# Two sets and two rounds in one tick of a fused convolution kernel

## The chip, the cores and the metric

The kernel runs on one core of a Trainium2 chip. The metric is the device time of one execution in microseconds (us), the median of several runs. The engines of a core are named as in the profile: PE (TensorE, matrix products), PEld (its weight loads), DVE (VectorE), ACT (ScalarE), POOL (GpSimd) and SP (SyncE, which here only starts transfers). All data are float32.

## The reference

The input `x` has 8 elements of 8 channels of 512x512. Two layers are computed, each added to its input. `_gn` is a normalisation over groups of two channels.

```python
x = x + _L0_conv_ref(_gn(x), T, X, weights1_ri, weights2_ri)   # spectral
x = x + _L1_conv_ref(_gn(x), K_local, Wp, bp, Wu, bu, Wg1, bg1, Wg2, bg2)

# layer 1, cut
grid = drive = x
for _ in range(15):                                  # STEPS
    mapped = 3.9 * grid * (1.0 - grid)
    local = conv3x3_depthwise(mapped, K_local)
    grid = 0.85 * (0.7 * mapped + 0.3 * local) + 0.15 * drive
cml_out = clip(grid, 0.0001, 0.9999)
h = relu(conv3x3(x, Wp, bp))                         # 8 -> 128 channels
nca_out = sigmoid(conv1x1(h, Wu, bu))                # 128 -> 8
gin = concatenate([x, cml_out, nca_out])
g = sigmoid(conv1x1(relu(conv3x3(gin, Wg1, bg1)), Wg2, bg2))
return g * cml_out + (1.0 - g) * nca_out
```

Layer 0 takes a few low frequencies of every second point of `x`, mixes the channels by weights and sums the waves back at all 512x512 points.

## The kernel before

The work of an element is cut into four kinds, which are interleaved in **ticks**. The order of the instructions on each engine is the order of the source (a helper, `keep_order`, fixes it).

- A **set** is one of the 15 steps for a fifth of the rows of half the channels. An element has 150 sets: 75 of its first half, 75 of its second. `convolve` does its products on PE, `settle` empties the two pairs of PSUM banks on DVE and squares the result on ACT. Every third step `renew` copies the rows that neighbouring slabs share. A set comes again five sets later.
- A **round** is 4 rows of the hidden layer: products from `cols`, relu to `h` (half on ACT, half on DVE), then the pointwise product, whose result is added up in `y` over four rounds. An element has 128 rounds.
- A **gate** is 12 rows of the last part, `conv` and `point`, for the element before the current one. There are 43 for an element.
- The **spectral pieces** compute layer 0 and the normalisation of the element after the current one. `layer0` is a generator and each `yield` ends a piece.

PSUM is four `pairs` of banks. A tick of before is one set (two pairs), one round (the other two), then a gate's conv, or its point, or up to two spectral pieces, and the round's pointwise product:

```python
pairs = [pp.tile([P, 2, N], F32, name=f"pair{i}") for i in range(4)]

def convolve(m, c0, step, ps):                       # L497
    for n, dx in enumerate((1, 0, 2)):
        for t in range(4):
            for h in range(4):
                at = slice(32 * h, 32 * h + 32)
                nc.tensor.matmul(
                    ps[h // 2][32 * t : 32 * t + 32, h % 2],
                    band[at, c0 + (t if step % 2 else h), dx],
                    m[at, t, dx : dx + N],
                    start=(n == 0), stop=(n == 2), tile_position=(32 * h, 32 * t),
                )

def settle(half, step, k, ps):                       # L552, L556
    m, d = half.m[k], half.d[k, step % 2]
    u = m[:, :, 1 : N + 1]
    for q in range(2):
        at = slice(2 * q, 2 * q + 2)
        nc.vector.scalar_tensor_tensor(
            u[:, at], ps[q], FLOOR, d[:, at], ALU.max, ALU.add
        )
        if step < STEPS:
            nc.scalar.square(u[:, at], u[:, at])
    # ... cut: a set's first and last steps, later(1, renew)

class Hidden:
    def round(self, ps, after):                      # L599, L605, L606
        # ... cut: which cols, the next load
        for n, (dx, lo, hi, at) in enumerate(SHIFTS):
            for g in range(4):
                p = slice(32 * g, 32 * g + 32)
                nc.tensor.matmul(
                    ps[g // 2][:, g % 2, lo:hi], w_p[p, dx, i % 2],
                    self.cols[p, i // 2, at : at + hi - lo],
                    start=(n == 0), stop=(n == 2), tile_position=(32 * g, 0),
                )
        self.h = wk.tile([P, 4, N], F32, tag="h", name="h", bufs=1)
        nc.scalar.activation(self.h[:, :2], ps[0], AF.Relu, bias=b_p)
        nc.vector.tensor_scalar(self.h[:, 2:], ps[1], b_p, 0.0, ALU.add, ALU.max)

    def point(self, ps):                             # L612, L618, L620
        i = self.n % 4
        for g in range(4):
            nc.tensor.matmul(
                ps[32 * g : 32 * g + 32], w_u[:, i], self.h[:, g],
                start=True, stop=True, tile_position=(0, 32 * g),
            )
        if i == 0:
            self.y = wk.tile([P, N], F32, tag="y", name="y", bufs=2)
            nc.scalar.copy(self.y, ps)
        else:
            nc.vector.tensor_tensor(self.y, self.y, ps, ALU.add)
        # ... cut: after four rounds sigmoid and store of y

class Gate:
    def conv(self, ps):                              # L662 on PE
        # ... 12 products of gin, tile_position=(0, 32 * j)
        # POOL: d - ng (L667); DVE: x1 (L668), relu of ps into mix (L672)
    def point(self, ps):                             # L677
        # one product; ACT: sigmoid (L678); POOL: d * g (L680); later(1, self.finish)
    def finish(self):                                # L686
        # DVE: one sum of three terms into mix; later(1, self.store)

def work(step, more, e, after, ps):
    if step:
        half, n, k = step
        convolve(half.m[k], half.c0, n - 1, ps[0])
        settle(half, n, k, ps[0])
    if more:
        e.hidden.round(ps[1], after)
    others.pieces([pair[:, 0] for pair in ps[0 if more else 1]])
    if more:
        e.hidden.point(ps[1][0][:, 0])
    tick()
```

`later(n, f)` runs `f` at the end of the n-th tick. Within an element all gates come first, the spectral pieces after them. The last element has only 48 rounds in its ticks with sets, and the rest of its rounds and its own gates follow in a tail without sets. Tiles of `sets` (15 slots) and `shared` (5 slots: `gin` and `mix` of gates, `x` of spectral pieces) are handed out by name.

Of the kernel before, what the change touches and what calls it, by code (L numbers as in the profile page):

```python
# [41 lines left out]
P = 128  # L42
# [12 lines left out]
ROUNDS, ROUNDS_LAST = 128, 48  # L55
SLAB, HALO, SETS = 32, 3, 5
SHARED = 5

# [66 lines left out]
def conv_layers(ctx: ExitStack, tc: tile.TileContext, a, out):  # L125
# [29 lines left out]
    def row(shape, name):  # L155
        return wk.tile(shape, F32, tag="row", name=name, bufs=3)
# [58 lines left out]
    def wave_table(name, pos, col, shift):  # L215
# [6 lines left out]
        u = row([8, N], "u")  # L222
# [8 lines left out]
        t = cp.tile([8, N], F32, name=name)  # L231
        nc.scalar.activation(t, u, AF.Sin, scale=6.283185)
        return t

    e1c = wave_table("e1c", "X", 0, 0.25)
    e1s = wave_table("e1s", "X", 0, None)
    e2 = wave_table("e2", "T", 1, waves[:, 2:3])


# [41 lines left out]
    def group_stats(st, n, bank):  # L281
# [5 lines left out]
        yield  # L287
# [8 lines left out]
        yield  # L296
# [6 lines left out]
        yield  # L303
        return mean, rstd, std

    def layer0(e, bank):

# [18 lines left out]
        yield  # L326
        mean, rstd, _ = yield from group_stats(st, G, bank)
# [9 lines left out]
        wmix = row([8, 2, C, C, 4], "wmix")  # L337
        nc.sync.dma_start(out=wmix, in_=a["wmix"])
        yield
# [10 lines left out]
        yield  # L350


        def total(q0, v0, q1, v1, op, name):
            ts = row([8, 2, C, C, 4], "ts")
            for i, (q, v) in enumerate(((q0, v0), (q1, v1))):
                nc.vector.tensor_tensor(
                    ts[:, i], f[:, :, q].unsqueeze(2).to_broadcast([8, C, C, 4]), wmix[:, v],
                    ALU.mult,
                )
            nc.vector.tensor_tensor(ts[:, 0], ts[:, 0], ts[:, 1], op)  # L360
            t = sm.tile([8, C, 4], F32, name=name)
            nc.vector.tensor_reduce(t, ts[:, 0].rearrange("k i o m -> k o m i"), AX.X, ALU.add)
            return t

        re = total(0, 0, 1, 1, ALU.subtract, "re")
        yield
        im = total(0, 1, 1, 0, ALU.add, "im")
        om = sm.tile([8, C, 2, 8], F32, name="om")
        s = 1.0 / (NS * NS)
        nc.vector.tensor_scalar(om[:, :, 0, 0:4], re, s, None, ALU.mult)  # L370
        nc.vector.tensor_scalar(om[:, :, 0, 4:8], im, s, None, ALU.mult)
        nc.vector.tensor_scalar(om[:, :, 1, 0:4], im, -s, None, ALU.mult)
        nc.vector.tensor_scalar(om[:, :, 1, 4:8], re, s, None, ALU.mult)
        yield


        def over_rows(c):
            ps = bank[-1]
            nc.tensor.matmul(ps[:8], om[:, c, 0], e1c, start=True, stop=False)
            nc.tensor.matmul(ps[:8], om[:, c, 1], e1s, start=False, stop=True)  # L380
# [6 lines left out]
        def close(g, st):  # L387

            mean, rstd, std = yield from group_stats(st, 1, bank)
            nc.vector.tensor_copy(means[:, 0, g : g + 1], mean)  # L390
            nc.vector.tensor_copy(means[:, 1, g : g + 1], std)
            for c in (2 * g, 2 * g + 1):
# [10 lines left out]
                yield  # L403
# [3 lines left out]
        closing = iter(())  # L407
        for c in range(C):
# [3 lines left out]
            for j in range(4):  # L412
# [3 lines left out]
                nc.vector.bn_stats(st[:, c % 2, j], xt[:, j])  # L416
                yield
                if j == 2 and c + 1 < C:
                    ty_next = over_rows(c + 1)
                    yield  # L420
                if next(closing, closing) is not closing:
                    yield
            if c % 2:
                closing = close(c // 2, st)
            if c + 1 < C:
                yield C + c + 1
        for _ in closing:
            yield
        back = e.back
# [3 lines left out]
        nc.vector.tensor_reduce(back, pick, AX.X, ALU.add)  # L433
# [7 lines left out]
    class Half:  # L441
# [22 lines left out]
        def prepare(self, n):  # L464

            for k in range(SETS):
                if n == k - 2:
                    self.square(k)
                if n == 2 * k - 5:
                    self.drive(k, 1)  # L470
            while n >= -10 and self.loads and (self.loads[0][2] or sets.free):
# [57 lines left out]
    def leave(m, k, half):  # L529
# [14 lines left out]
        later(2, store)  # L544

    def settle(half, step, k, ps):
# [3 lines left out]
        for q in range(2):  # L550
# [3 lines left out]
            )  # L554
            if step < STEPS:
# [12 lines left out]
    class Hidden:  # L568
# [4 lines left out]
        def __init__(self, e):  # L573
            self.e, self.tiles, self.loaded, self.n = e, deque(), 0, 0
# [12 lines left out]
        def round(self, ps, after):  # L587

            i = self.n % 4
# [14 lines left out]
            self.h = wk.tile([P, 4, N], F32, tag="h", name="h", bufs=1)  # L604
            nc.scalar.activation(self.h[:, :2], ps[0], AF.Relu, bias=b_p)  # L605
            nc.vector.tensor_scalar(self.h[:, 2:], ps[1], b_p, 0.0, ALU.add, ALU.max)  # L606

        def point(self, ps):

            i = self.n % 4  # L610
            for g in range(4):
                nc.tensor.matmul(  # L612
                    ps[32 * g : 32 * g + 32], w_u[:, i], self.h[:, g],
                    start=True, stop=True, tile_position=(0, 32 * g),
                )
            if i == 0:
                self.y = wk.tile([P, N], F32, tag="y", name="y", bufs=2)
# [3 lines left out]
            self.n += 1  # L621
            if i == 3:
                y, r0 = self.y, 4 * self.n - 16
# [10 lines left out]
    class Gate:  # L634
# [39 lines left out]
        def point(self, ps):  # L674
# [6 lines left out]
            later(1, self.finish)  # L681

        def finish(self):
# [5 lines left out]
            later(1, self.store)  # L689
# [12 lines left out]
    class Element:  # L702


        def __init__(self, b):
            self.b, self.rows = b, 0
            self.xn, self.cml, self.nca = planes[b % 2]
# [23 lines left out]
        def spectral(self, ps):  # L731

            if not self.pieces:
                return
            if self.need is not None and now[0] < self.at.get(self.need, now[0]) + 3:
                return
            self.bank.append(ps)
            self.need = next(self.pieces, self)
            if self.need is self:
                self.pieces = None  # L740
            self.bank.clear()

    class Others:


        def __init__(self):
            self.before, self.after, self.limit = None, None, 2
            self.loaded, self.convolved = deque(), deque()

        def feed(self):  # L750
            e = self.before
            while e and e.gates and len(self.loaded) < self.limit and len(shared.free) > 1:
# [5 lines left out]
            if self.after and not (e and e.gates):  # L758
                self.after.fetch()

        def busy(self):
            return self.before.gates or self.loaded or self.convolved

        def pieces(self, banks):

            if self.convolved:
                self.convolved.popleft().point(banks[0])
            elif self.loaded and self.loaded[0].at + 2 <= now[0]:
                self.convolved.append(self.loaded.popleft())
                self.convolved[0].conv(banks[0])  # L770
            elif self.after:
                for ps in banks:
                    self.after.spectral(ps)
# [5 lines left out]
    for i in range(2):  # L779
# [11 lines left out]
    for c, t in enumerate(xs_first):  # L791
        e.x[c], e.at[c], e.at[C + c] = t, -3, -3
    turns = cycle(pair[:, 0] for pair in pairs)
    while e.pieces:
        e.spectral(next(turns))
# [3 lines left out]
    for n in range(-10, 0):  # L799
# [5 lines left out]
    def work(step, more, e, after, ps):  # L805

        if step:
            half, n, k = step
            convolve(half.m[k], half.c0, n - 1, ps[0])
            settle(half, n, k, ps[0])  # L810
        if more:
            e.hidden.round(ps[1], after)
        others.pieces([pair[:, 0] for pair in ps[0 if more else 1]])
        if more:
            e.hidden.point(ps[1][0][:, 0])
        tick()

    halves = pairs[:2], pairs[2:]
    for b in range(B):
        after = Element(b + 1) if b + 1 < B else None  # L820
        others.after = after
        rounds = ROUNDS if after else ROUNDS_LAST
        for t in range(2 * TICKS):
            half, behind = (e.first, e.second) if t < TICKS else (e.second, after and after.first)
            n = t % TICKS
            assert not after or t != 2 * TICKS - 10 or not after.pieces
            half.prepare(n)
            if behind:
# [72 lines left out]
```

## Time and profile before

| | before |
|---|---|
| time, median of 3 runs | 11553.06 us (11540.5 to 11559.4) |
| span of the profiled run | 11555.9 us |
| first product of a set | 238.7 us after the start |
| end of the last set | 11037.5 us |
| mean granted PE clock | 0.974 |
| transferred | 1353.10 MB, mean 117 GB/s |

A group line of the profile names the line of the source, the engine, the operation, the output and inputs, and the count. Then come the busy time and the mean length of one in ns, and then the engine's idle time just before these instructions with what ended most of it. A timeline line has the start in us, the length, the engine and the instruction. Products overlap in PE, so the time that a block of them takes is read from its start to the start of the next block. 1200 sets and 1024 rounds are spread over the 11.5 ms.

### The profile page before, as it was taken

What the parts mean: (1) busy time and instruction counts of PE and PEld (TensorE: products, weight loads), DVE (VectorE), ACT (ScalarE), POOL (GpSimd) and SP (SyncE); (2) the same over time, 40 slices, a digit from 0 to 9 for tenths busy, and PEclk for the clock granted to TensorE, in tenths of its full rate; (3) what the DMA queues carried; (4) which work ended last, traced back from release to release, by engine and by line L of the source; (5) the groups of instructions that cost most, each with busy time, mean ns of one, the idle gap of its engine ahead of it and who ended that gap; (6) DMA issues with size and microseconds to landing.
All of it is one profiled execution on the core that took longest, in us unless ns stands there. A gap on an engine that the chain in (4) does not pass through costs nothing. (4 is left out here: it accounts for less than half of the span.)

```text
span 11555.9 us, 349769 instructions
## 1 busy us (share of the span) xinstructions
PE 10228.8 (89%) x158864; PEld 3755.7 (33%) x158864; DVE 6597.8 (57%) x6779; ACT 4243.8 (37%) x4444; POOL 1733.2 (15%) x1285
## 2 busy tenths in 40 slices
PE   5988889899898989989899898988989899897789
PEld 2332233233333333333333333333333233332222
DVE  4654456566565655656565655656656566555455
ACT  1333333334333334334333333433433334333322
POOL 0010021300113011120112102121021200122012
PEclk9999999999999999999999999999999999999999
DMA  3222045632556335562355514564145632555067
GB/s 107 85 72 60 29 126 135 158 108 75 139 130 161 102 99 126 130 163 82 112 126 138 161 64 121 130 152 137 60 130 134 162 109 72 148 140 135 20 167 179
DMA packets 624855, 1353.10 MB, mean 117 GB/s; under 512 B 72452, under 2 KB 72580, under 8 KB 593356
## 3 DMA queue, kind: packets, MB, share of 16 engines
q1 hardware_dynamic: 559712, 1161.94, 38.3%
q10 hardware_dynamic: 63660, 168.77, 5.9%
q8 instruction: 1249, 20.46, 0.8%
q14 instruction: 234, 1.92, 0.1%
HBM read 992.29 MB, written 268.66 MB: 109 GB/s over the span
## 5 line engine op out<-in xcount | busy, mean ns | idle before, releaser
L497 PE MATMUL pair<-m,band 32*32 32x512 f32 x115200 | 4462.1, 617 | 249.3 <-DVE m L552 140.3
L556 ACT ACTIVATE m<-m 128x1024 f32<-128x1024 f32 x2240 | 2365.9, 1057 | 5188.4 <-DVE m L552 4866.4
L599 PE MATMUL pair<-cols,w_p 32*128 32x511 f32 (+1 forms) x24576 | 2933.7, 606 | 32.8 <-ACT mix L678 18.2
L497 PEld LDWEIGHTS pair<-m,band 32*32 32x32 f32 x115200 | 1797.5, 104 | 2877.1 <-issue 1454.9
L552 DVE SCALAR_TENSOR_TENSOR m<-pair,dO 128x1024 f32<-128x1024 f32 x1280 | 1507.1, 1219 | 1517.1 <-PE pair L497 1361.2
L552 DVE SCALAR_TENSOR_TENSOR m<-pair,dE 128x1024 f32<-128x1024 f32 x1120 | 1318.8, 1219 | 1267.4 <-PE pair L497 1177.1
L612 PE MATMUL pair<-h,w_u 128*32 128x512 f32 x8192 | 1177.3, 625 | 856.5 <-ACT h L605 855.4
L599 PEld LDWEIGHTS pair<-cols,w_p 32*128 32x128 f32 x24576 | 1163.1, 185 | 1819.2 <-issue 1606.8
L606 DVE TENSOR_SCALAR h<-pair,b_p 128x1024 f32<-128x1024 f32 x1024 | 1313.1, 1282 | 551.8 <-PE pair L599 496.0
L605 ACT ACTIVATE h<-pair,b_p 128x1024 f32<-128x1024 f32 x1024 | 1126.0, 1100 | 911.4 <-PE pair L599 509.3
L680 POOL TENSOR_TENSOR mix<-mix 96x512 f32<-96x512 f32 x344 | 437.8, 1273 | 4765.0 <-ACT mix L678 3929.8
L662 PE MATMUL pair<-gin,w_g 128*32 128x511 f32 (+1 forms) x8256 | 982.9, 609 | 54.5 <-DVE m L552 52.7
L560 POOL TENSOR_SCALAR dO<-dO 128x2048 f32<-128x2048 f32 x80 | 436.2, 5452 | 3945.5 <-DVE m L552 3945.5
L620 DVE TENSOR_TENSOR y<-y,pair 128x512 f32<-128x512 f32 x768 | 526.3, 685 | 833.7 <-PE pair L612 826.5
L686 DVE SCALAR_TENSOR_TENSOR mix<-mix,back 96x512 f32<-96x512 f32 x344 | 619.6, 1801 | 395.5 <-POOL mix L680 350.5
L612 PEld LDWEIGHTS pair<-h,w_u 128*32 128x32 f32 x8192 | 197.5, 110 | 1618.9 <-ACT h L605 1453.2
L662 PEld LDWEIGHTS pair<-gin,w_g 128*32 128x32 f32 x8256 | 238.3, 111 | 751.0 <-issue 467.1
L667 POOL TENSOR_TENSOR mix<-mix 96x512 f32<-96x512 f32 x344 | 441.8, 1284 | 162.2 <-DMA mix<-nca 80.9
L677 PE MATMUL pair<-mix,w_g 128*96 128x512 f32 x688 | 379.1, 633 | 7.0 <-DVE mix L672 7.0
L624 ACT ACTIVATE y<-y,b_u 128x512 f32<-128x512 f32 x256 | 184.8, 722 | 524.2 <-DVE y L620 524.1
L672 DVE TENSOR_SCALAR mix<-pair,b_g 128x512 f32<-128x512 f32 x344 | 257.1, 747 | 159.4 <-PE pair L662 156.4
L668 DVE SCALAR_TENSOR_TENSOR mix<-mix,back 96x512 f32<-96x512 f32 x344 | 308.3, 896 | 0.0
(85 smaller groups left out, 2943.1 us busy)
## 6 DMA issues: line engine op xcount, KB each, us to landing
gin<-xn SPq DMA_DIRECT2D x344, 384.0 KB
cols<-xn SPq DMA_DIRECT2D x256, 512.0 KB
x<-in_x SPq DMA_DIRECT2D x120, 1024.0 KB
gin<-cml SPq DMA_DIRECT2D x344, 320.0 KB
gin<-nca SPq DMA_DIRECT2D x344, 320.0 KB
dE<-xn ACTq DMA_DIRECT2D x320, 256.0 KB
dO<-xn ACTq DMA_DIRECT2D x320, 256.0 KB
mix<-xn SPq DMA_DIRECT2D x344, 192.0 KB
```

What stands on the lines that cost most here:

```text
L497: nc.tensor.matmul(ps[h // 2][32 * t : 32 * t + 32, h % 2], band[at, c0 + (t if step % 2 else h), dx], m[at, t, dx : dx + N], start=(n == ...
L552: nc.vector.scalar_tensor_tensor(u[:, at], ps[q], FLOOR, d[:, at], ALU.max, ALU.add)
L556: nc.scalar.square(u[:, at], u[:, at])
L599: nc.tensor.matmul(ps[g // 2][:, g % 2, lo:hi], w_p[p, dx, i % 2], self.cols[p, i // 2, at : at + hi - lo], start=(n == 0), stop=(n == 2), ...
L605: nc.scalar.activation(self.h[:, :2], ps[0], AF.Relu, bias=b_p)
L606: nc.vector.tensor_scalar(self.h[:, 2:], ps[1], b_p, 0.0, ALU.add, ALU.max)
L612: nc.tensor.matmul(ps[32 * g : 32 * g + 32], w_u[:, i], self.h[:, g], start=True, stop=True, tile_position=(0, 32 * g),)
L620: nc.vector.tensor_tensor(self.y, self.y, ps, ALU.add)
L662: nc.tensor.matmul(ps[32 * j : 32 * j + 32, lo:hi], gband[:, dx], gin[:, j, at : at + hi - lo], start=(n == 0), stop=(n == 2), tile_positi ...
L667: nc.gpsimd.tensor_tensor(d, d, ng, ALU.subtract)
L680: nc.gpsimd.tensor_tensor(d, d, mix[: GR * C, 2], ALU.mult)
L686: nc.vector.scalar_tensor_tensor(o, o, self.e.back[: GR * C, 0:1], x1, ALU.add, ALU.add)
```

## The change

A tick becomes two sets, each with its own two pairs of banks, then two rounds, then the gate or the spectral pieces, then the two pointwise products, and at the end the gate's point or more spectral pieces. An element has 75 ticks, 64 of them with rounds. It is meant to let the work that empties one block's banks lie beside the next block's products.

`settle` is now a generator, so that the relu of the first round is placed before the second square of the second set on ACT. The gate's last sum (`finish`) comes in the following tick after the eviction of a set, and its store at once. Gates are loaded until tick 27 of an element, then the spectral pieces run from tick 26 on, and the remaining gates follow, so that no gates stand in the middle of an element; for that there are three sets of planes in DRAM instead of two. `h` has two buffers, `y` one and `row` two instead of three. The two products of `over_rows` are merged into one. Pieces are marked `LATER` (the first in its group only) or `LONG` (two large ones per tick at most).

```diff
+GATES_TO, SPECTRAL_FROM = 27, 26
+LONG, LATER = -1, -2
...
-        return wk.tile(shape, F32, tag="row", name=name, bufs=3)
+        return wk.tile(shape, F32, tag="row", name=name, bufs=2)
...
         def over_rows(c):
             ps = bank[-1]
-            nc.tensor.matmul(ps[:8], om[:, c, 0], e1c, start=True, stop=False)
-            nc.tensor.matmul(ps[:8], om[:, c, 1], e1s, start=False, stop=True)
+            nc.tensor.matmul(ps[:8], om[:, c], e1, start=True, stop=True)
...
-        later(2, store)
+        later(1, store)
     def settle(half, step, k, ps):
...
             )
+            if q:
+                yield
             if step < STEPS:
                 nc.scalar.square(u[:, at], u[:, at])
...
-            self.h = wk.tile([P, 4, N], F32, tag="h", name="h", bufs=1)
-            nc.scalar.activation(self.h[:, :2], ps[0], AF.Relu, bias=b_p)
-            nc.vector.tensor_scalar(self.h[:, 2:], ps[1], b_p, 0.0, ALU.add, ALU.max)
+            h = wk.tile([P, 4, N], F32, tag="h", name="h", bufs=2)
+            nc.scalar.activation(h[:, :2], ps[0], AF.Relu, bias=b_p)
+            next(settled, None)
+            nc.vector.tensor_scalar(h[:, 2:], ps[1], b_p, 0.0, ALU.add, ALU.max)
+            self.hs.append((self.n - 1, h))
...
-                self.y = wk.tile([P, N], F32, tag="y", name="y", bufs=2)
+                self.y = wk.tile([P, N], F32, tag="y", name="y", bufs=1)
...
-            later(1, self.finish)
...
-            later(1, self.store)
+            self.store()
...
-            self.xn, self.cml, self.nca = planes[b % 2]
+            self.xn, self.cml, self.nca = planes[b % 3]
...
+        def feed(self, t):
+            e, after = self.before, self.after
+            spectral = after and after.pieces
+            while e and e.gates and (t < GATES_TO or not spectral):
...
+        def first(self, banks):
+            self.longs = 0
+            n = 0
             if self.convolved:
-                self.convolved.popleft().point(banks[0])
-            elif self.loaded and self.loaded[0].at + 2 <= now[0]:
-                self.convolved.append(self.loaded.popleft())
-                self.convolved[0].conv(banks[0])
+                self.point(banks[1])
+                n = 2
+            if self.loaded and self.loaded[0].at < now[0]:
+                g = self.loaded.popleft()
+                g.conv(banks[0])
+                self.convolved.append(g)
+                n = n or 1
+            elif n == 0 and self.after:
+                n = self.spectral(banks)
+            return n
+
+        def second(self, banks, wait):
+            if self.convolved:
+                if not wait:
+                    self.point(banks[0])
             elif self.after:
-                for ps in banks:
-                    self.after.spectral(ps)
+                self.spectral(banks)
...
+    def work(sets, rounds, e, after):
+        settled = iter(())
+        for (half, step, k), ps in zip(sets, (pairs[:2], pairs[2:])):
+            convolve(half.m[k], half.c0, step - 1, ps)
+            next(settled, None)
+            settled = settle(half, step, k, ps)
+            next(settled)
+            others.finish()
+        others.finish()
+        for ps in (pairs[:2], pairs[2:])[:rounds]:
+            e.hidden.round(ps, after, settled)
+        next(settled, None)
+        a, b, c, d = (pair[:, 0] for pair in pairs)
+        n = others.first([a, b])
+        if rounds:
+            e.hidden.point(c if n else a)
+        if rounds > 1:
+            e.hidden.point(d if n else c)
+        others.second([pair[:, 1] for pair in pairs[2:]], rounds == 0)
         tick()
```

## The prediction

> **What bounds the kernel now.** I read the busy shares first, then the costliest groups, then who waits for whom, and last single ticks in the timeline.
>
> ```profile
> PE 10228.8 (89%) x158864; PEld 3755.7 (33%) x158864; DVE 6597.8 (57%) x6779; ACT 4243.8 (37%) x4444; POOL 1733.2 (15%) x1285
> ```
>
> TensorE (PE) is busy 89% of the span, VectorE (DVE) 57%. So PE's order of work sets the time, and the question is what its 11% of idle time and the seams inside its busy time are.
>
> ```profile
> L552 DVE SCALAR_TENSOR_TENSOR m<-pair,dO 128x1024 f32<-128x1024 f32 x1280 | 1507.1, 1219 | 1517.1 <-PE pair L497 1361.2
> ...
> L612 PE MATMUL pair<-h,w_u 128*32 128x512 f32 x8192 | 1177.3, 625 | 856.5 <-ACT h L605 855.4
> ...
> L686 DVE SCALAR_TENSOR_TENSOR mix<-mix,back 96x512 f32<-96x512 f32 x344 | 619.6, 1801 | 395.5 <-POOL mix L680 350.5
> ```
>
> The middle line is the main one: before the pointwise product (L612) PE stands idle for 856 us in all, and the releaser is the relu `h` on ScalarE (ACT). That is most of PE's idle time (11556 - 10229 = 1327 us). The list of waits gives the same, and shows that the wait of the sets' products (L497) for the eviction is small:
>
> ```profile
> PE pair L612 <- ACT h L605: 855.4, 706, 13.4
> ...
> PE pair L497 <- DVE m L552: 140.3, 166, 2.5
> ```
>
> Now one tick of before with a spectral piece, in the timeline (start, duration, then the instruction):
>
> ```profile
> 4016.28 3.40 PE L497 MATMUL pair<-m,band 32*32 32x512 f32 x96
> ...
> 4018.03 0.75 PEld L497 LDWEIGHTS pair<-m,band 32*32 32x32 f32 x31 [0.30 <-issue]
> 4019.62 0.31 PEld L599 LDWEIGHTS pair<-cols,w_p 32*128 32x128 f32 x8 [0.84 <-issue]
> 4019.62 2.85 PE L599 MATMUL pair<-cols,w_p 32*128 32x512 f32 x24
> 4019.69 2.36 DVE L552 SCALAR_TENSOR_TENSOR m<-pair,dE 128x1024 f32<-128x1024 f32 x2 [2.06 <-PE pair L497]
> ...
> 4022.29 1.05 PE L414 MATMUL pair<-e,ty 8*128 8x512 f32 x2
> ...
> 4023.05 1.10 ACT L605 ACTIVATE h<-pair,b_p 128x1024 f32<-128x1024 f32 x1
> ...
> 4024.20 1.07 PE L612 MATMUL pair<-h,w_u 128*32 128x512 f32 x8 [0.85 <-ACT h L605]
> ...
> 4025.19 3.41 PE L497 MATMUL pair<-m,band 32*32 32x512 f32 x96
> ```
>
> From start to start: set 3.34 us, round 2.67, spectral piece 1.91 (its own work about 0.9, the rest is the wait for `h`), pointwise product 0.99; the tick is 8.91. The eviction of a set takes 2.36 on DVE and ACT's relu comes last because it stands behind both squares. And a pair of ticks with one gate:
>
> ```profile
> 4417.82 2.85 PE L599 MATMUL pair<-cols,w_p 32*128 32x512 f32 x24
> 4420.60 1.10 PE L677 MATMUL pair<-mix,w_g 128*96 128x512 f32 x2
> 4422.39 1.07 PE L612 MATMUL pair<-h,w_u 128*32 128x512 f32 x8 [0.69 <-ACT h L605]
> 4423.39 3.40 PE L497 MATMUL pair<-m,band 32*32 32x512 f32 x96
> 4426.72 2.85 PE L599 MATMUL pair<-cols,w_p 32*128 32x512 f32 x24
> 4429.51 2.78 PE L662 MATMUL pair<-gin,w_g 128*32 128x512 f32 x24
> 4432.10 1.04 PE L612 MATMUL pair<-h,w_u 128*32 128x512 f32 x8
> ```
>
> Gate product 1.79 (with its wait), gate convolution 2.59, product after it about 1.05; with two sets and two rounds the pair takes 18.7. The convolution is long enough to hide the relu, so there is no wait beside it. Ticks with neither gate nor piece also take 8.9: their whole wait, about 1.8, is bare.
>
> **What the Trainium skill says.** "TensorEngine Tiling (Array Packing)", Key Properties: changing the tiling mode, not just the tile, drains the engine. The trace agrees in kind: the first weight load of the 32x128 round comes after 0.84 us without loads, where loads inside the round are 0.22 apart. The same page, PSUM Bottleneck: tiling speeds up the products but not the emptying of PSUM. Also seen: a set is 3.34 on PE and 2.36 on DVE, which leaves little. "TensorE: Matmul & The Clock Gate", the table at its head: ScalarE and VectorE are strict first-in first-out. The trace shows it in the relu behind the squares; it is why the order of instructions is the change.
>
> **The change, part by part.** All lengths are PE's, start to start.
>
> Two sets in a row: inside a set the starts of single products come in six waves, at 0, 0.45, 1.08, 1.53, 2.15 and 2.60 us. After the first two, whose weights were loaded in advance, two waves take 1.07. If the second set just continues, the first costs 3 x 1.07 = 3.22 and the second 3.34: 6.56 for two, saving only 0.12. I choose this; if the seam vanishes wholly it would be near 5.9.
>
> Two rounds: six waves of 0.43 make 2.57, then 2.79 with the seam: 5.36. Two pointwise products: 0.86 + 1.0. Spectral pieces: about 0.9 each, mostly two to a tick. Gate product without a wait: 1.0.
>
> The relu of round 1 now runs during round 2. That of round 2 has the gate or piece, and the first product, beside it. So the wait for `h` goes from nearly all ticks; with nothing between, 1.79 - 0.86 = 0.93 stays.
>
> A new wait: in gate ticks DVE does eviction of set A, then the gate's last sum (L686, 1.8), then eviction of set B. A is done at 3.4 after the tick's start; 3.4 + 2.4 + 1.8 + 2.4 = 10.0 until B's banks are empty. Round 2 wants them at 6.56 + 2.6 = 9.2. So 0.8 to 0.9 of stall in each gate tick. Without a gate the chain is 6.6 + 2.4 = 9.0 and just fits.
>
> Ticks of the new kind:
> - gate, with rounds: 6.56 + 5.36 + 0.9 + 2.6 + 1.86 + 1.0 = 18.3 (before: 18.7 for the same work)
> - spectral, with rounds: 6.56 + 5.36 + 1.86 + two or three pieces, about 2.4 = 16.2 (before 17.8)
> - neither: 6.56 + 5.36 + 1.86 + 0.93 = 14.7 (before 17.8)
> - without rounds: 11.2 with a gate (its bank must be emptied before set A), 9.5 with pieces, 7 with neither.
>
> One element has 75 ticks, 64 with rounds. The 43 gates take 37 with and 6 without; the spectral part about 22 and 4 (at two large pieces a tick, 8 first transforms take 4 ticks and 32 sums 16, the small pieces in between some 6); 5 and 1 are left. 37 x 18.3 + 6 x 11.2 + 22 x 16.2 + 4 x 9.5 + 5 x 14.7 + 7 = 1219. How far such a sum falls short I take from before:
>
> ```profile
> 4339.10:5727.80 1388.70, 1257.30 (x19860) 465.59 (x19858) 825.89 (x833) 530.29 (x556) 216.83 (x161) 0.98 0.47 122
> ```
>
> This is one element's stretch (length, then busy time by engine, granted clock 0.98). Its 150 ticks, sorted by what they hold and each kind counted at its most frequent length, sum to about 1300; some 85 us more come from ticks of 12 to 19 us near the change of halves, where ACT stands behind loads of `dE` and `dO`, and from the clock. I keep 75 of it: gates no longer run there. So 1294 for an inner element.
>
> The sum: start to the first set 240, as before; element 0, without gates, 42 x 14.7 + 7 x 7 + 22 x 16.2 + 4 x 9.5 = 1060, with 50 for disturbances 1110; six inner elements 7764; the last, with 24 round ticks and 43 gates, 14 x 18.3 + 29 x 11.2 + 10 x 14.7 + 22 x 7 = 882, with 60 more 942; the tail of 43 gates and 40 pairs of rounds, 5.36 + 2.6 + 1.86 + 1.0 = 10.9 each, about 485 (before 519). Together 10,541, say 10,540: 8.8% less.
>
> What lies beside other work: three planes instead of two cost no time; `row` and `y` with one buffer less are used once in one or two ticks, so their stores are done; the gate's earlier store and the single product per channel in `over_rows` (64 x 0.85 = 55 us, within the pieces' estimate) are small.
>
> **The rivals.**
> 1. The set's seam is the drain and vanishes between two sets: 0.6 less in each of 600 ticks, 360 us: 10,180. For it: no loads in 0.84 us at the switch. Against: waves inside a set already slow down after the first two.
> 2. DVE becomes the chain. In gate ticks it has 4.7 + 1.8 + 2.6 + 1.6 + 1.0 = 11.7 of 18.3, so it isn't full, but its order matters: if the gate's sum has to wait for POOL, or bank waits are taken at both rounds, 1 to 2 us more in some 300 ticks: 11,000. For it: the eviction chain has no slack left. Against: POOL's product lies a tick earlier.
> 3. Transfers. A set's rows at slab ends (L527) must land before it is used again, formerly four ticks of 9 us, now one tick of 16 to 18 and a part. The DMA share is 0.47 in an inner element and would rise to 0.5. If loads of gates (1.6 MB each) hold these up, the gain shrinks to a few per cent: 11,100 to 11,400. Against: no such wait for `m<-m` is among the large ones today, and a whole tick remains.
>
> **Range and chances.** The middle is the sum. Rival 1 gives the lower end (10,180 with some luck in the disturbances, 10,080), rival 2 with a little of rival 3 the upper end, 11,060. A gain under 2% (over 11,322) needs rival 3 to strike in most ticks; slower than 11,784 needs a stall of 2 us in each of 600 ticks beyond those I count. Faster 0.92, within 2% 0.05, slower 0.03.
>
> **What would show it.** Right: the idle time before L612 falls from 856 to under 200 us; set to set is 3.2 and two sets with the seam 6.5 to 6.6; gate ticks near 18.3 with an idle time at L599 that DVE's eviction (L552 of before) releases; ticks with neither near 14.7; elements near 1290. Wrong: round 2 waits much over 0.9, set products wait for `m<-m` transfers, or a tick of two sets starts the second after 2.7 us instead of 3.2. The clearest failure would be an element's length that stays near 1388.

## The result and the profile after

| | before | after |
|---|---|---|
| time, median | 11552.94 us | 10718.39 us (10691.58 to 10728.41) |
| ratio to before | | 0.9275, 95% interval 0.9257 to 0.9294 |
| span of the profiled run | 11555.9 us | 10714.4 us |
| mean granted PE clock | 0.974 | 0.964 |
| first product of a set after | 238.7 us | 244.1 us |
| an inner element | about 1389 us | 1312.7 us (1305.0 to 1318.9) |

The kernel is 7.25% faster. The predicted time was 10,540 us, the range 10,080 to 11,060. The parts of the span are 244 to the first set, 1099 for element 0, 7876 for elements 1 to 6, 1003 for the last with sets and 486 for the tail up to its last product; together 10,708, and 6 more to the end of the span.

Below is the line of busy shares of the kernel after, which answers to the first one shown of before.

```profile
PE 9762.8 (91%) x158736; PEld 4467.4 (42%) x158736; DVE 6212.8 (58%) x6779; ACT 4290.4 (40%) x4444; POOL 1723.5 (16%) x1285
```

PE's idle time fell from 1327 to 952 us (10714.4 - 9762.8), a loss of 375. But PE's busy time fell by more, 466 us, although the products of sets, rounds and gates are the same. Busy time contains the seams between blocks, and the products that start late because their weights do. The share alone (89% to 91%) shows almost nothing of an 8% change.

The groups of the kernel after (busy and mean ns, then the idle time before and its releaser):

```profile
L509 PE MATMUL pair<-m,band 32*32 32x512 f32 x115200 | 4222.8, 615 | 341.0 <-issue 147.7
...
L629 PE MATMUL pair<-h,w_u 128*32 128x512 f32 x8192 | 1042.3, 610 | 139.2 <-ACT h L619 138.3
...
L422 PE MATMUL pair<-e,ty 8*128 8x512 f32 x512 | 312.1, 733 | 134.0 <-ACT ty L391 54.2
...
L701 DVE SCALAR_TENSOR_TENSOR mix<-mix,back 96x512 f32<-96x512 f32 x344 | 308.7, 908 | 103.1 <-POOL mix L696 103.1
```

The pointwise product (L629, formerly L612) waits 139 us, no longer 856, and its busy time fell from 1177 to 1042. The sets (L509, formerly L497) are busy 239 us less and idle 92 more. Part is given back: the idle time before the waves of layer 0 (L422, formerly L414) rose from 5.5 to 134. The gate's last sum (L701, formerly L686) has halved: a mean of 908 ns, where it was 1801.

One gate tick of the kernel after, in the timeline (start, length, engine, instruction):

```profile
4370.55 6.58 PE L509 MATMUL pair<-m,band 32*32 32x512 f32 x192
...
4373.96 2.35 DVE L564 SCALAR_TENSOR_TENSOR m<-pair,dE 128x1024 f32<-128x1024 f32 x2 [2.55 <-PE pair L509]
...
4377.06 5.43 PE L613 MATMUL pair<-cols,w_p 32*128 32x512 f32 x48
4377.13 2.35 DVE L564 SCALAR_TENSOR_TENSOR m<-pair,dE 128x1024 f32<-128x1024 f32 x2 [0.82 <-PE pair L509]
...
4380.01 1.11 ACT L619 ACTIVATE h<-pair,b_p 128x1024 f32<-128x1024 f32 x1 [0.56 <-PE pair L613]
...
4382.41 2.78 PE L678 MATMUL pair<-gin,w_g 128*32 128x512 f32 x24
4382.58 1.12 ACT L619 ACTIVATE h<-pair,b_p 128x1024 f32<-128x1024 f32 x1 [0.51 <-PE pair L613]
...
4385.01 1.90 PE L629 MATMUL pair<-h,w_u 128*32 128x512 f32 x16
...
4386.84 1.10 PE L693 MATMUL pair<-mix,w_g 128*96 128x512 f32 x2
```

The next tick starts at 4387.87. So this one takes 17.32: two sets 6.51, two rounds 5.35, gate convolution 2.60, two products 1.83, gate product 1.03. No block of products in it has a wait noted. The relu of the first round (ACT at 4380.01) lies beside the second round, that of the second (4382.58) beside the gate's convolution, and the eviction of the first set (DVE at 4373.96) beside the second set.

### The profile page after: what moved, and what is told of

It is laid out like the page before. It is cut to its first block, busy times and chain, and to the rows that moved or that the text cites. A ratio compares the mean times of both kernels' runs of the same rounds, so it can differ in the third digit from the quotient of the medians.

```text
span 10714.4 us, 349371 instructions
## 1 busy us (share of the span) xinstructions
PE 9762.8 (91%) x158736; PEld 4467.4 (42%) x158736; DVE 6212.8 (58%) x6779; ACT 4290.4 (40%) x4444; POOL 1723.5 (16%) x1285
## 5 line engine op out<-in xcount | busy, mean ns | idle before, releaser
L509 PE MATMUL pair<-m,band 32*32 32x512 f32 x115200 | 4222.8, 615 | 341.0 <-issue 147.7
L509 PEld LDWEIGHTS pair<-m,band 32*32 32x32 f32 x115200 | 2289.8, 104 | 2158.9 <-issue 1097.8
L613 PE MATMUL pair<-cols,w_p 32*128 32x511 f32 (+1 forms) x24576 | 2856.7, 601 | 37.6 <-issue 20.0
L564 DVE SCALAR_TENSOR_TENSOR m<-pair,dO 128x1024 f32<-128x1024 f32 x1280 | 1507.7, 1219 | 1350.0 <-PE pair L509 1240.1
L613 PEld LDWEIGHTS pair<-cols,w_p 32*128 32x128 f32 x24576 | 1343.7, 186 | 1565.2 <-issue 1119.9
L564 DVE SCALAR_TENSOR_TENSOR m<-pair,dE 128x1024 f32<-128x1024 f32 x1120 | 1318.9, 1219 | 1073.9 <-PE pair L509 991.3
L629 PE MATMUL pair<-h,w_u 128*32 128x512 f32 x8192 | 1042.3, 610 | 139.2 <-ACT h L619 138.3
L629 PEld LDWEIGHTS pair<-h,w_u 128*32 128x32 f32 x8192 | 247.1, 111 | 811.4 <-issue 403.6
L422 PE MATMUL pair<-e,ty 8*128 8x512 f32 x512 | 312.1, 733 | 134.0 <-ACT ty L391 54.2
L701 DVE SCALAR_TENSOR_TENSOR mix<-mix,back 96x512 f32<-96x512 f32 x344 | 308.7, 908 | 103.1 <-POOL mix L696 103.1
```

What stands on the lines that cost most here:

```text
L509: nc.tensor.matmul(ps[h // 2][32 * t : 32 * t + 32, h % 2], band[at, c0 + (t if step % 2 else h), dx], m[at, t, dx : dx + N], start=(n == ...
L564: nc.vector.scalar_tensor_tensor(u[:, at], ps[q], FLOOR, d[:, at], ALU.max, ALU.add)
L613: nc.tensor.matmul(ps[g // 2][:, g % 2, lo:hi], w_p[p, dx, i % 2], self.cols[p, i // 2, at : at + hi - lo], start=(n == 0), stop=(n == 2), ...
L629: nc.tensor.matmul(ps[32 * g : 32 * g + 32], w_u[:, i], h[:, g], start=True, stop=True, tile_position=(0, 32 * g),)
```

## The experiments

All times are medians; the ratio is to the kernel before on the same chip. A diff is against the kernel after unless it says otherwise.

### The rounds taken apart

The tick keeps its two sets, but the second round stands behind the gate or the pieces, and each round's product again follows one block later. (The lines with `#` stand for lines left out.)

```diff
-        for ps in (pairs[:2], pairs[2:])[:rounds]:
-            e.hidden.round(ps, after, settled)
-        next(settled, None)
-        # first([a, b]), point, point, second([pairs 2, 3])
+        if rounds:
+            e.hidden.round(pairs[:2], after, settled)
+        next(settled, None)
+        others.first([c, d])
+        if rounds:
+            e.hidden.point(a)
+        if rounds > 1:
+            e.hidden.round(pairs[2:], after, settled)
+        others.second([pair[:, 1] for pair in pairs[:2]], rounds == 0)
+        if rounds > 1:
+            e.hidden.point(c)
```

> The changed kernel with the rounds apart again: two sets, round, gate or pieces, product, round, the rest, product. Theory H (the gain is the wait for h, which the second round hides): the idle time before the pointwise product returns from 139 us to 700 or more, and the time is 11,350 to 11,550. Rival S (the gain is the fewer changes between kinds of products on PE): only the seams of the second round and second product return, some 0.25 us in 512 ticks, so 10,800 to 10,900.

Measured: 11405.96 us, ratio 0.9873 (0.9856 to 0.9890). Of the gain of 835 us some 690 are gone, as theory H has it. From the waits of this kernel:

```profile
PE pair L629 <- ACT h L619: 642.4, 590, 22.3
```

The wait for `h` is back, 504 us more than in the kernel after, if a little under the 700 expected. The time is lost where nothing covers the relu: the median tick with rounds but neither gate nor pieces goes from 15.0 to 17.9, one with a gate's convolution only from 17.8 to 18.3. Seams alone would have cost every kind alike. PE's idle time as a whole grew by 336, since other waits shrank, and its busy time by 369. In that the rounds (L613) went from 2857 to 3122 and the products (L629) from 1042 to 1296: blocks that stand singly have more seams, and products whose `h` comes late are stretched. How the 369 divide between the two isn't measured. So the pair of rounds, and not the pair of sets, carries most of the gain.

### The late product in the old tick

The kernel before, with one edit, of which the main lines are shown (the comment is added): a round's product comes after the *next* round's products, into a bank of the set's pair that was just emptied.

```diff
-            e.hidden.round(ps[1], after)
+            e.hidden.round(ps[1], after, ps[0][0][:, 1])   # the round before it: point
         others.pieces([pair[:, 0] for pair in ps[0 if more else 1]])
-        if more:
-            e.hidden.point(ps[1][0][:, 0])
```

> The kernel before, ticks of one set and one round as they were, but a round's pointwise product is done after the next round's products. Theory H: PE no longer waits for h, so most of 856 us goes, less some waits of the next set for the sum into y: 10,850 to 11,050. Rival S: the number of changes between kinds of products is as before, so 11,450 to 11,600.

Measured: 12549.19 us, ratio 1.0866 (1.0836 to 1.0897), a miss for every theory. From the waits of this kernel:

```profile
PE pair L616 <- DVE m L552: 281.8, 199, 2.7
PE pair L497 <- ACT mix L681: 247.8, 232, 7.1
PE pair L497 <- DVE mix L675: 223.0, 231, 3.3
```

The wait for `h` fell to 11.8 us, as it should. But now the product (L616) waits for the set's eviction, and the next set (L497) for the gate's last readers of its banks, because no product lies between them any more. Hiding `h` is not enough; with four pairs of banks the wait moves to the banks. It doesn't tell the pairing of rounds from that of sets, since its own new waits hide either.

### The relu behind both squares

```diff
-            if q:
-                yield
             if step < STEPS:
                 nc.scalar.square(u[:, at], u[:, at])
+            if q:
+                yield
```

> The changed kernel with both squares of a set ahead of the relu on ACT. If the place of the relu matters, round 1's relu comes 1.05 us later and ticks without gate and pieces, and those that fill the first banks, get up to 1 us longer: 10,850 to 11,100. If a whole round and more lies between the relu and its product anyway: 10,700 to 10,760, no difference.

Measured: 10728.18 us, ratio 0.9293 (0.9269 to 0.9316), which can't be told from the kernel after. A whole second round, 2.7 us, lies between the relu and what needs it, so a square of 1.05 us ahead of it costs nothing that shows. This part of the change is idle.

### The loop order inside a set

The order of the starts inside a set was one possible reason for its slow waves; here the loop over `h` is the outer one and that over `t` the inner.

```diff
-            for t in range(4):
-                for h in range(4):
+            for h in range(4):
+                for t in range(4):
```

> The changed kernel with a set's 16 products of one shift issued row group by row group (h outside, t inside) instead of in turn over the row groups. If the slow waves inside a set (1.07 us for two instead of 0.86) come from the order in which weight loads can be pulled ahead, they change with it: shorter gives 10,000 to 10,300, longer loads of one row group behind each other give 11,000 to 11,500. If the waves are bound by the issue of 64 instructions: no change, 10,700 to 10,760.

Measured: 10726.88 us, ratio 0.9288 (0.9267 to 0.9309). No change: the groups of 16 products start at the same times inside a set, too (0, 0.45, 0.88, 1.31, 1.76, 2.37 us in the first). So the order isn't the cause; that the issue of 64 instructions is, isn't shown by this.

### GpSimd beside the gate's last sum

The sum had shrunk from 1.80 to 0.91 us. In the trace of before, POOL's product of another gate runs beside it:

```profile
4424.22 1.28 POOL L667 TENSOR_TENSOR mix<-mix 96x512 f32<-96x512 f32 x1
...
4424.30 1.76 DVE L686 SCALAR_TENSOR_TENSOR mix<-mix,back 96x512 f32<-96x512 f32 x1
```

I sorted all 344 sums of each kernel by whether a POOL instruction runs beside them. Before, 313 had one for over 0.6 us and took 1.75 (median), 30 had none and took 0.75. After, 51 had one (1.74), 280 none (0.74). So the sum takes as long as ever beside such a neighbour; the neighbour has gone. Two kernels put it back. The first starts an additional multiplication on POOL at the sum:

```diff
             x1, o = (self.mix[: GR * C, q] for q in range(2))
+            spare = self.mix[: GR * C, 2]
+            nc.vector.memset(spare[:, 0:1], 0.0)
+            nc.gpsimd.tensor_tensor(spare, spare, spare, ALU.mult)
```

> The changed kernel with one more POOL multiplication of 96x512 (its result isn't used) placed so that it runs beside the gate's last sum on DVE. If the sum's 1.75 us of the kernel before came from POOL running beside it: its mean goes from 0.91 to about 1.75 us, round 2 waits some 0.8 us more in 300 gate ticks, and the time is 10,900 to 11,000, as my gate tick of 18.3 had it. If the sum's length has another cause: it stays at 0.9 and the time at 10,720 to 10,760.

Measured: 10748.47 us, ratio 0.9294 (0.9278 to 0.9311), an interval that overlaps that of the kernel after: no effect is shown. The groups of this kernel say why:

```profile
L703 POOL TENSOR_TENSOR mix<-mix 96x512 f32<-96x512 f32 x344 | 517.3, 1508 | 914.3 <-DVE mix L702 886.6 <-DMA mix<-cml 7.4 <-DMA gin<-xn 6.9
L704 DVE SCALAR_TENSOR_TENSOR mix<-mix,back 96x512 f32<-96x512 f32 x344 | 294.0, 864 | 103.7 <-issue 103.7
```

DVE began first in nearly all cases and kept its time (0.74 us in the median, 0.86 on average); it was POOL that grew, to 1.51 us, where its instructions of this size take 1.28. So the experiment was not the one I meant. The second starts a POOL multiplication of twice the size before the second part of set A's eviction, so that it is under way when the sum comes:

```diff
             at = slice(2 * q, 2 * q + 2)
+            if q:
+                others.beside()
...
+        def beside(self):
+            for g in self.pointed:
+                spare = g.mix[: GR * C, 2:4]
+                nc.vector.memset(spare[:, :, 0:1], 0.0)
+                nc.gpsimd.tensor_tensor(spare, spare, spare, ALU.mult)
```

> The changed kernel with an unused POOL multiplication of 96x1024 that now starts before the second eviction of set A, so that it is already running when the gate's last sum comes to DVE. If DVE has to wait for a POOL instruction that began earlier: the sum's mean goes from 0.91 to 1.7 to 2.2 us, round 2 waits 0.8 to 1.2 us more in 300 gate ticks, 10,950 to 11,080; this is the stall of my gate tick. If DVE isn't held up by POOL: 10,720 to 10,770.

Measured: 10915.97 us, ratio 0.9445 (0.9426 to 0.9464), 198 more than after. A group and a wait of this kernel:

```profile
L703 DVE SCALAR_TENSOR_TENSOR mix<-mix,back 96x512 f32<-96x512 f32 x344 | 608.7, 1780 | 101.7 <-POOL mix L698 101.7
```

```profile
PE pair L615 <- DVE m L566: 62.3, 56, 3.0
```

The sum is at 1.78 again. It ends 0.55 us after POOL's instruction, as it did before, although POOL's takes 1.89 here and 1.27 there (medians): DVE waits for POOL's end. And the rounds (L615 here) wait for the eviction of set B (L566), 62 us where the kernel after has 1.4. In ticks with a gate's convolution the two rounds took 5.94 on average and take 6.60 now. Spread over the 301 additional POOL instructions it is 198 / 301 = 0.66 us each, a little less than the stall of 0.8 to 0.9 that I had predicted.

### The loads of `dE` and `dO` moved from ACT to SP

The ticks of an element with the same number are alike, so their mean shows where time is lost: half of the gate ticks with rounds take under 17.8, but tick 36 took 28.8, tick 71 28.7, tick 73 25.8 and tick 1 26.7. This is tick 71 of element 3 in the timeline of the kernel after, PE, DVE, ACT and ACT's queue of transfers (ACTq):

```profile
5188.86 5.43 PE L613 MATMUL pair<-cols,w_p 32*128 32x512 f32 x48
...
5195.22 6.99 ACTq L472 DMA_DIRECT2D dO<-xn  x4
...
5202.25 2.95 ACT L570 ACTIVATE m<-m 128x1024 f32<-128x1024 f32 x3 [18.85 <-DMA dO<-xn]
...
5205.11 1.09 ACT L619 ACTIVATE h<-pair,b_p 128x1024 f32<-128x1024 f32 x1
...
5206.25 3.77 PE L629 MATMUL pair<-h,w_u 128*32 128x512 f32 x16 [11.97 <-ACT h L619]
```

ACT computes nothing for 18.85 us, and in this time it starts four loads of `dO`. The 6.99 is the stretch from the first start to the end of the last; each start alone takes 0.31 to 0.32. What they wait for stands in the trace. Each transfer of the kernel signals one of eight semaphores, and each of these starts waits until the transfer that used its semaphore before has landed. Here that is a gate's transfer, started by SP (SPq is its queue):

```profile
5183.72 0.45 SPq L663 DMA_DIRECT2D gin<-cml  x1
5184.22 0.46 SPq L663 DMA_DIRECT2D gin<-nca  x1
5187.42 0.32 SPq L668 DMA_DIRECT2D mix<-xn  x1
...
5191.73 0.30 SPq L668 DMA_DIRECT2D mix<-nca  x1
```

These four landed at 5195.20, 5197.60, 5198.69 and 5201.88, and ACT's four loads started 0.02 to 0.03 us later (5195.22, 5197.62, 5198.72, 5201.90). So ACT stands behind transfers that its next computation doesn't need. In the whole run 252 of the 640 loads of `dE` and `dO` start so, after waits of some 600 us together. Only after the loads come three squares and the relu, and PE's product has waited 11.97 for the relu. The profile puts the wait down to `h`. It does so for other products too:

```profile
PE pair L678 <- ACT h L619: 88.3, 17, 20.1
...
PE pair L422 <- ACT h L619: 50.1, 6, 9.2
```

With the 138 before L629, PE waits 277 us for the relu in the kernel after. The loads go to SP:

```diff
             while n >= -11 and self.loads and (self.loads[0][2] or sets.free):
-                self.load(nc.scalar)
+                self.load(nc.sync)
```

> The changed kernel with the loads of dE and dO started by SP instead of ACT. Theory A (the long ticks of 20 to 29 us at the change of half and element come from ACT standing behind its own transfer starts): they shrink to 17 to 20, some 40 us in each element, 10,300 to 10,500, and ACT's waits for dE and dO vanish. Rival D (the transfers themselves are too slow there, the DMA share is 0.8 to 0.9): the waits move to other instructions and the time stays at 10,650 to 10,800, or is longer since SP's other transfers stand behind these.

Measured: 10506.23 us, ratio 0.9104 (0.9090 to 0.9117), 212 less than the kernel after and at the upper edge of theory A's band. Tick 71 fell to 14.3 and tick 36 to 16.0, tick 73 to 20.2; tick 1 remained at 30.0. From the waits of this kernel:

```profile
PE pair L678 <- DMA gin<-nca: 66.9, 11, 12.6
PE pair L629 <- ACT h L619: 50.0, 117, 4.0
```

The long waits for `h` are gone: 50 us in all remain of the 277, and the longest is 4.0, where it was 20.1. A wait of 67 for the gates' loads, which now stand behind these on SP, has come, so rival D has a part too.

The same edit on the kernel before:

> The kernel before with nothing changed but the loads of dE and dO started by SP instead of ACT. If ACT's standing behind its transfer starts costs the old tick what it costs the new one (211 us there): 11,300 to 11,400, and the change is worth the same on top of it. If the old tick, in which ACT's relu is waited for in nearly every tick, loses more by it: 11,100 to 11,250. If less, because its waits lie elsewhere: 11,450 to 11,550.

Measured: 11422.73 us, ratio 0.9899 (0.9883 to 0.9916), 117 less, between the two bands expected. The wait for `h` there is 758.6 us, 97 less than before. So the loads in ACT's order were about a ninth of that wait; the rest stays, and goes only with the order of the tick. With the loads on SP in both, the change is 10506 / 11423, a gain of 8.0%.

### The place of the pause

The gates pause from tick 6 instead of 27, so that gates instead of spectral pieces run at the change of halves.

```diff
-GATES_TO, SPECTRAL_FROM = 27, 26
+GATES_TO, SPECTRAL_FROM = 6, 5
```

> The changed kernel with the pause of the gates moved from ticks 27 to 52 to ticks 6 to 31, so that gates run while the second half's tiles are loaded (ticks 32 to 40). If the place of the pause matters because the loads of gates and of tiles collide: the ticks 32 to 40 get some 30 to 60 us longer per element, 10,900 to 11,150. If not: 10,650 to 10,800.

Measured: 10866.01 us, ratio 0.9411 (0.9395 to 0.9428), 148 more than after: a cost, though less than expected. Ticks 35 to 37 take 38.3, 27.9 and 30.3. Is that only the loads in ACT's order again? The same with the loads on SP:

> Loads of dE and dO started by SP, and the pause of the gates at ticks 6 to 31, so that gates run while the second half is loaded. If the place of the pause matters only through ACT's standing behind its transfer starts: as with loads on SP alone, 10,480 to 10,540. If it matters through the transfers themselves: 100 to 200 us more, 10,600 to 10,720, with waits for gin and m.

Measured: 10685.44 us, ratio 0.9238 (0.9215 to 0.9262), 179 more than with the loads on SP alone. So the pause doesn't only keep ACT free; gates beside the change of halves cost the same without them.

### One gate's load at a time, and in what order

With the loads on SP, at most one gate is loaded in a tick while an element follows:

```diff
                 self.loaded.append(g)
+                if self.after:
+                    break
```

> Loads of dE and dO started by SP, and at most one gate loaded in a tick instead of up to two. With loads on SP alone the second tick of an element takes 30 us, 9.7 of them a wait for gin of a gate behind the tiles and a second gate. If the second gate is what stands in the way: 6 to 10 us less in two ticks of each element, 10,380 to 10,460. If the tiles alone fill the queue: no change, 10,490 to 10,530.

Measured: 10454.86 us, ratio 0.9053 (0.9027 to 0.9079): the best kernel here, 264 less than the kernel after, and 51 less than with the loads on SP alone. The time is as expected, but the reason isn't: tick 1 is 28.6 (was 30.0), and the wait for `gin` is still 62 us. In a last kernel the gates' loads also start ahead of those of the next sets:

```diff
+            others.feed(t)
             e.first.prepare(2 * t)
...
-            others.feed(t)
```

> As with one gate a tick, and the gate's loads are started before those of dE and dO. If gin is what the second tick waits for: its wait goes, 10,330 to 10,430. If the tiles then come too late: waits of POOL and ACT for dE and dO reach PE, 10,450 to 10,600.

Measured: 10519.24 us, ratio 0.9093 (0.9066 to 0.9120), no better than the loads on SP alone. The order of these starts isn't what tick 1 suffers from. What made the 51 us stays open. In tick 1 the DMA engines are nearly full, wherever the starts stand: in the kernel with one gate a tick they are busy for 0.92 to 0.95 of the time from 3866 to 3897 us, around tick 1 of element 3, and for 0.50 in a stretch of usual gate ticks (4100 to 4300). This fits a tick held by the transfers themselves, as rival D had it for the loads on SP; no run takes any of them out. A later first load of the gates was not tried, as the 75 ticks of an element leave no room for it.

## Why the prediction held, and where it was off

**The wait for `h`: right.** The step "So the wait for `h` goes from nearly all ticks" predicted under 200 us of idle time; it is 139 before that product, or 277 with the waits for the relu before other products, most of which go when the loads leave ACT. And taking the rounds apart brings 504 of it back and takes 82% of the gain.

**The seam of the sets: right in sum, wrong inside.** Predicted were 6.56 for two sets, as 3.22 and 3.34; measured 6.51, as 2.82 and 3.69. The step "3 x 1.07" took the slow pace for all of the first set. But as in a single set of before, its groups of 16 products start at 0, 0.45, 0.88, 1.31, 1.76 and 2.37 us, early ones included; only the second set is slow throughout, and has the seam. My check, "starts the second after 2.7 us instead of 3.2", would have taken that for rival 1: the seam behind the first set does go (2.82 instead of 3.34), but the second takes 0.35 longer than a single one. The pair saves only 0.17 against two single sets (6.68), not the 0.6 of rival 1, which falls. "TensorEngine Tiling (Array Packing)", Key Properties, says that a change of mode drains the engine; here the change from sets to rounds again shows 0.84 us without weight loads, but leaving out half of these changes gained 0.17 us a pair. What sets the slow waves isn't settled; the loop order doesn't.

**The ticks.** I sorted the 75 ticks of elements 1 to 6 by what they hold:

| kind | predicted | measured, mean | median |
|---|---|---|---|
| gate, with rounds | 37 x 18.3 = 677 | 36 x 18.8 = 677 | 17.8 |
| spectral, with rounds | 22 x 16.2 = 356 | 19 x 18.7 = 356 | 17.9 |
| neither, with rounds | 5 x 14.7 = 74 | 9 x 16.6 = 149 | 15.0 |
| gate, no rounds | 6 x 11.2 = 67 | 7 x 11.3 = 79 | 10.4 |
| pieces or neither, no rounds | 38 + 7 = 45 | 4 ticks, 51 | |
| left over | 75 | in the means | |
| element | 1294 | 1313 | |

Of the 177 us by which the sum of 10,541 fell short, six inner elements make 112, at 19 each, and the last element 61. Two errors met in the inner ones. **The gate's stall was too large.** The step "3.4 + 2.4 + 1.8 + 2.4 = 10.0 until B's banks are empty" took the sum at 1.8 us, its length beside POOL. In its new place it is 0.74, or 0.91 on average, the chain is 9.1, and the stall goes; the most frequent gate tick is 17.4, which is 18.3 less that stall, and the median 17.8. That the mean of 18.8 brings the product to the predicted 677 is luck. The length itself could have warned me: DVE's sum into `y`, over 128 lanes instead of 96, takes 0.68. The Trainium skill says it in "SBUF — State Buffer", on the two separate sides: for a DVE instruction with two inputs in SBUF, as this sum has, a pair of ports shared with GpSimd is an exclusive lock, held for the whole instruction by whoever began. The trace agrees: 1.74 beside POOL's 1.28, 0.74 without, the end 0.55 us after POOL's, and in both directions it is the later of the two that grows.

**The disturbances were too small.** "I keep 75 of it: gates no longer run there" was wrong on two counts. The waits at the change of halves came as much from the loads that stand in ACT's order as from the gates, and those loads stayed; moving them is worth 212 us in the whole kernel. And at the end of an element gates do run again, beside the next element's first loads: ticks 71 to 73 average 28.7, 21.8 and 25.8. "DMA: Bandwidth & Descriptors", on issuing engines, says that transfers run on the same 16 engines whoever starts them, and that more starters save only the start's own time. Here the start itself is small, too, 0.3 to 0.4 us in the median; the loads are the same, but on ACT each start with its wait for an earlier transfer stood ahead of the relu. The excess of all ticks is 1313 - 1219 = 94 of my plain sum, though that sum already had 33 (37 x 0.9) for a stall that didn't come. A part of it has no known cause: 148 us of idle time before the sets' products in the whole run have no releaser in the profile (4 before). In these stretches the DMA engines are busy for 0.69 of the time, from the first set to the last for 0.47, so transfers may have a share in them.

**Spectral ticks** with rounds are 17.9 in the median, not 16.2, as the products of layer 0 wait more: the idle time before its groups on PE is 326 us in all, before 121. There are fewer of them, so their term of the sum came out right by luck. Of the 55 us named for the merged product of `over_rows` little is left: its busy time fell from 145 to 88, the idle time before it rose from 4 to 52.

**The other parts.** Start (244 against 240), element 0 (1099 against 1110) and tail (486 against 485) are as predicted. The last element took 1003, not 942: its 16 ticks with gate and rounds average 22.8, where I had taken 14 at 18.3; one of them, at the change of halves, takes 50.5 (34.1 with the loads on SP). In this element gates run beside the tiles' loads there, as in the kernel with the early pause; the rest was not tried.

**Rival 2** (DVE as the chain) appears only when POOL's work is laid on the sum, as the 10916 us show; **rival 3** (transfers) came in another form than I gave it: not as `m<-m` waits (8 us) but as loads whose starts waited on ACT for other transfers, 212 us.

## What to carry to other kernels

Pair blocks of the same kind, so that each block's reader works beside the other's products; look for room in the banks first, as a late product without a free bank loses more than it hides. Don't start transfers that may be held up from an engine whose next instruction is on the path: the wait appears under that engine's name, and only its queue's own line in the timeline tells. Before you move an instruction, ask what ran beside it when its length was measured.

## What was unexpected in the hardware

- A DVE sum of 96x512 takes 0.74 us alone and 1.74 beside a POOL multiplication that started 0.1 us earlier, and ends 0.55 us after it; if DVE starts first it keeps its time and POOL goes from 1.28 to 1.51.
- Of two sets in a row the first takes 2.82 and the second 3.69, seam included, while a single set took 3.34.
- A start of one of these loads takes ACT 0.3 to 0.4 us in the median, but in one tick ACT stood still for 18.85: its four starts waited for semaphores that transfers started by SP had still to signal, and went off 0.02 to 0.03 us after these had landed.
